# Local attention on one core: keys-first weights between the projection's halves, outputs turned in front of queries and keys, the halo scaled early

## The chip, the cores and the metric

The kernel runs on one core of a Trainium2 chip as one program. The metric is device time in microseconds (us). Before the change three runs took 5033.6, 5040.5 and 5043.14 us, median 5040.5.

## The reference, cut to what matters

Two stages, each with a first half (attention of its own kind) and a second half of local-attention layers. The change touches the second halves only: 6 layers of 16 heads with windows of 32 tokens (stage L0), then 2 layers of 8 heads with windows of 64 (stage L1). The data are 2 sequences of 2048 tokens by 128 features there, all in fp32. One layer computes:

```python
h = shift_token(x)                       # half of the features come from the token before
q, k, v = split(h @ Wqkv)                # heads of 64
q, k = l2norm(q) * qs, l2norm(k) * ks
q, k = rotary(q) * scale, rotary(k) / scale
sim = 8 * q_window @ [k_previous_window, k_window].T   # masked
o = softmax(sim) @ [v_previous_window, v_window]
x = x + o @ Wo
h = layernorm(shift_token(x))            # feed-forward
x = x + ((h @ Wa + ba) * gelu(h @ Wg + bg)) @ W2 + b2
```

L1's first half (a causal linear attention with its own feed-forward) is computed block by block among the tiles at the seam between the two stages.

## The kernel before, in words

After L0's first half, `local_models` walks through 256 tiles: 8 layers, 16 tiles of 128 tokens, 2 sequences (the sequence is the inner loop). Activations stay in SBUF with features on partitions (`hs`). Each tile goes through these steps, one function each; the names in brackets are the tiles that the profile shows.

- `project(j, u)` multiplies tokens by one kilocolumn of Wqkv (`ps_qk`, L871, four array passes of 512 columns). ScalarE squares the result (`sq`, L873), VectorE multiplies it by the rotary tables in two instructions (L881 into `r`, L886 into `t`), GpSimd adds the two (L892). L0 has two such halves (u = 0, 1: `nu` is 2), L1 one (`nu` is 1). After the last half VectorE reduces the squares (L897) and computes an inverse root in nine small instructions (L167 to L180, the result is `rq_y`, the scratch is the PSUM tile `ps_qk` itself); GpSimd scales `r` with it (L904).
- `values` projects V (`ps_v`, L951), ScalarE copies it out (`vn`, L952), and SyncE's DMA queue arranges windows in `v2` (L961 to L964, ten DMAs in an L0 tile).
- `turn` transposes queries and keys (`ps_turn`, L923); ScalarE copies them to `qT` and `kT` (L926, L928). Its end fills the keys' halo, the window before the tile, from the same sequence's last tile: one ScalarE activation that scales it (L934), or a memset by GpSimd at the start of a sequence (L932).
- `scores` puts the mask in PSUM with two bf16 matmuls (`ps_s`, L982), adds 64 small score products (L991; they use 64 by 32 parts of the array), and VectorE takes the maximum (L999) and subtracts it (L1001). `weights_exp` is ScalarE's exp (L1008), `weights_norm` a sum, a reciprocal (VectorE, L1015, L1016) and a scaling on GpSimd (L1017).
- `keys_first_` transposes the weights (`ps_pT`, L1026), and ScalarE copies them to `pT` in two instructions (L1027).
- `mix` multiplies weights with values (`ps_o`, L1043, again small array parts); ScalarE copies to `on` (L1049).
- `turn_out` transposes that (`ps_oT`, L1059), ScalarE copies to `oT` (L1060); `project_out` multiplies by Wo (`ps_y`, L1071), VectorE adds the residual (L1077).
- `feed_forward` queues six closures for each 512 tokens (`steps`): centre (`ps_c`, L1096, squared by ScalarE into `fsq`, L1098), variance (`ps_var`, L1107), scale (`ps_r`, L1120), gate and up (`ps_f`, L1141, with ScalarE's Gelu at L1151 and VectorE's product at L1158), down (`ps_fy`, L1166). Each round of the main loop takes two of them. `linear` and `output` queue closures of the seam and of the end in the same way (`lsteps`).

The tiles are software pipelined. Round i of the main loop computes the scores of tile i+1, the projection of tile i+3, weights, mix and output of tile i, and values and turning of tile i+2. Each round emits, in this order: scores(i+1) with exp and normalising; project(i+3, 0); one feed-forward step; project(i+3, 1) in L0 only; keys_first_(i) and values(i+2); mix(i) and turn(i+2); turn_out(i); one feed-forward step; project_out(i).

This is the order in which the source emits; a scheduler then gives each engine its own fixed order, which stays near the emitted one but lets a later instruction pass one that it expects to wait. Each engine runs its list strictly in order. PSUM is shared by two pools: `wide` (2 buffers of two banks: scores, projection halves, gate and up) and `bank` (4 buffers of one bank: everything else). A buffer comes free when its last reader is done. In SBUF, `pT` and `oT` share one buffer, `kT` has three, `vn` three, `v2` two.

Of the kernel before, what the change touches and what calls it, by code (L numbers as in the profile page):

```python
# [11 lines left out]
F32 = mybir.dt.float32  # L12
BF16 = mybir.dt.bfloat16
I32 = mybir.dt.int32
AF = mybir.ActivationFunctionType
# [57 lines left out]
def tile_kernel(ctx: ExitStack, tc: tile.TileContext, a: dict, out: bass.AP):  # L73
# [634 lines left out]
    def local_models(mA, mB, hs0):  # L708
# [141 lines left out]
        def tables(g, t):  # L850
            cs = wk.tile([128, 2, DH], F32, name="cs", bufs=2)
            nc.sync.dma_start(cs[:, 0], a["cos"][:, t, :])
            nc.sync.dma_start(cs[:, 1], a["sin"][:, t, :])
            tb = wk.tile([128, 2, 2, DH], F32, name="tb", bufs=3)
            for j in range(2):
                nc.gpsimd.tensor_tensor(
                    tb[:, j], fac[g][:, j], bc(cs[:, j].unsqueeze(1), (128, 2, DH)), ALU.mult
                )
            tabs[g, t] = tb


        def project(i, u):
            g, b, t = tiles[i]
            m, _ = layers[g]
            H, units = m.H, m.units
            tb = tabs[g, t]
            hw = hs[0][:, b, t * 128:(t + 1) * 128]
            pq = wide("qk")
            for j in range(2):
                js = slice(512 * j, 512 * j + 512)  # L870
                nc.tensor.matmul(pq[:, js], lhsT=hw, rhs=wts[g, u][:, js], start=True, stop=True)  # L871
            sq = wk.tile([128, 1024], F32, name="sq", bufs=2)
            nc.scalar.activation(sq, pq, AF.Square)  # L873
            r = wk.tile([128, 1024], F32, name=f"r{u}", bufs=2)
            t2 = wk.tile([128, 1024], F32, name="t2", bufs=1)
            same = units[u][0][0] == units[u][1][0]
            for e in range(1) if same else range(2):
                s = units[u][e][0]
                hn = 16 if same else 8
                es = slice(512 * e, 512 * e + 64 * hn)  # L880
                nc.vector.tensor_tensor(  # L881
                    r[:, es].rearrange("p (h d) -> p h d", d=DH),
                    pq[:, es].rearrange("p (h d) -> p h d", d=DH),
                    bc(tb[:, 0, s].unsqueeze(1), (128, hn, DH)), ALU.mult,
                )
                nc.vector.tensor_tensor(  # L886
                    t2[:, es].rearrange("p (h s d) -> p h s d", s=2, d=32),
                    pq[:, es].rearrange("p (h s d) -> p h s d", s=2, d=32)[:, :, ::-1, :],
                    bc(tb[:, 1, s].rearrange("p (s d) -> p s d", s=2).unsqueeze(1),
                       (128, hn, 2, 32)), ALU.mult,  # L890
                )
            nc.gpsimd.tensor_tensor(r, r, t2, ALU.add)  # L892
            st[i]["r", u], st[i]["sq", u] = r, sq
            if u == len(units) - 1:

                for v in range(len(units)):
                    nc.vector.tensor_reduce(  # L897
                        pq[:, 16 * v:16 * v + 16],
                        st[i].pop(("sq", v)).rearrange("p (h d) -> p h d", d=DH), AX.X, ALU.add,
                    )  # L900
                y = rsqrt_quick([pq[:, k * 32:k * 32 + 2 * H] for k in range(4)], 2 * H, wk)
                for v in range(len(units)):
                    rv = st[i]["r", v].rearrange("p (h d) -> p h d", d=DH)
                    nc.gpsimd.tensor_tensor(  # L904
                        rv, rv, bc(y[:, 16 * v:16 * v + 16].unsqueeze(2), (128, 16, DH)), ALU.mult
                    )

        def turn(i, u):

            g, b, t = tiles[i]  # L910
            m, _ = layers[g]
            W, NPR = m.W, m.NPR
            if u == 0:
                q = wk.tile([128, 1024], F32, name="qT")
                st[i]["q"] = q[:, 0:NPR * 128].rearrange("p (c i) -> p c i", c=NPR)
                k = wk.tile([128, 1280], F32, name="kT", bufs=3)
                st[i]["k"] = k[:, 0:NPR * (W + 128)].rearrange("p (c i) -> p c i", c=NPR)
            r = st[i].pop(("r", u))
            for e, (s, pb) in enumerate(m.units[u]):
                p = bank("turn")  # L920
                for c in range(4):
                    cs = slice(512 * e + 128 * c, 512 * e + 128 * c + 128)
                    nc.tensor.transpose(p[:, c * 128:(c + 1) * 128], r[:, cs], ident)  # L923
                pv = p.rearrange("p (c i) -> p c i", c=4)
                if s == 0:
                    nc.scalar.copy(st[i]["q"][:, 4 * pb:4 * pb + 4, :], pv)  # L926
                else:
                    nc.scalar.copy(st[i]["k"][:, 4 * pb:4 * pb + 4, W:W + 128], pv)  # L928
            if u == len(m.units) - 1:
                k = st[i]["k"]  # L930
                if t == 0:
                    nc.gpsimd.memset(k[:, :, 0:W], 0.0)  # L932
                else:
                    nc.scalar.activation(  # L934
                        k[:, :, 0:W], m.last_k[b][:, :, 128:128 + W], AF.Identity, scale=m.back
                    )
                m.last_k[b] = k

        def values(i):
            g, b, t = tiles[i]  # L940
# [78 lines left out]
        def keys_first_(i):  # L1019
            sm = st[i].pop("p")  # L1020
            pT = wk.tile([128, 2, 4, 128], F32, tag="pT", name="pT")
            for q in range(2):
                p = bank("pT")
                for c in range(4):
                    cs = slice(512 * q + 128 * c, 512 * q + 128 * c + 128)
                    nc.tensor.transpose(p[:, c * 128:(c + 1) * 128], sm[:, cs], ident)  # L1026
                nc.scalar.copy(pT[:, q].rearrange("p c i -> p (c i)"), p)  # L1027
            st[i]["pT"] = pT
# [60 lines left out]
        def lstep():  # L1089
            if lsteps:  # L1090
                lsteps.pop(0)()
# [362 lines left out]
        for i in range(-3, n):  # L1454
            j = i + 3
            lstep()
            if 0 <= i + 1 < n:
                scores(i + 1)
                weights_exp(i + 1)
                weights_norm(i + 1)  # L1460
            more = False
            if j < n:
                g, b, t = tiles[j]
                jj = j % per
                nu = len(layers[g][0].units)
                more = g < last
                if g == second and t % 4 == 0:
                    while (b, t // 4) not in ready:
                        lstep()
                project(j, 0)  # L1470
                if more and jj == 4:
                    load_proj(g + 1, 0)
                if more and jj == 6 and g + 1 == second:
                    models[1].consts()
                if jj == 6 and g == second - 1:
                    linear_consts()
                if more and jj == 8:
                    factors(g + 1)
                    if 2 == 2:
                        load_out(g + 1)  # L1480
                if more and jj == 18:
                    load_ff(g + 1)
                if more and jj == 22:
                    fold_ff(g + 1)
                if more and jj == per - 1:
                    load_proj(g + 1, 1)
                lstep()
            step()
            if j < n and nu == 2:
                project(j, 1)  # L1490
                if more and jj == per - 1 and g + 1 < second:
                    load_proj(g + 1, 2)
            if j < n and b == B - 1 and j + 1 < n:
                tables(*tiles[j + 1][::2])
            lstep()
            if i >= 0:
                keys_first_(i)
            if 0 <= i + 2 < n:
                values(i + 2)
            lstep()  # L1500
            if i >= 0:
                mix(i)
            if 0 <= i + 2 < n:
                for u in range(len(layers[tiles[i + 2][0]][0].units)):
                    turn(i + 2, u)
            lstep()
            if i >= 0:
                turn_out(i)
            step()
            lstep()  # L1510
            if i >= 0:
                g, b, t = tiles[i]
                project_out(i)
                if 2 == 1 and i % per == per - 1 and g < last:
                    load_out(g + 1)
                if t % 4 == 3:
                    feed_forward(g, b, t // 4)
# [74 lines left out]
```

## Time and profile before

| what | value |
| --- | --- |
| three runs | 5033.6, 5040.5, 5043.14 us |
| profiled execution, its own time | 5053.27 us |
| its span, first to last instruction | 5051.4 us |
| granted TensorE clock, mean | 0.959 |
| stretch 650 to 3590 us (L0's layers): granted clock | 1.00 |
| in that stretch of 2940 us, busy: TensorE / VectorE / ScalarE / GpSimd | 2878.59 / 2379.62 / 1794.23 / 1870.56 us |
| stretch 3590 to 4400 us (seam with the linear attention): clock, TensorE / VectorE busy of 810 us | 0.96, 752.90 / 554.02 us |
| stretch 4400 to 5052 us (L1's layers alone): clock, TensorE / VectorE busy of 652 us | 0.98, 602.36 / 516.60 us |

How to read the profile. PE is TensorE's matmuls, PEld its weight loads, DVE VectorE, ACT ScalarE, POOL GpSimd, SP the DMA-issuing SyncE. "ps_o<-v,pT" is the output and inputs of an instruction, "L1043" its line. A busy TensorE isn't TensorE at its peak: matmuls overlap, and the times used below are therefore the distances between the starts of consecutive groups. The profiled execution took 12.8 us more than the median of the three runs.

### The profile page before, as it was taken

How to read it: one execution, taken by the hardware profiler on the slowest of the kernel's cores; microseconds unless marked ns; L12 is line 12 of the kernel's file. 1: busy time of each engine (PE TensorE's matmuls, PEld its weight loads, DVE VectorE, ACT ScalarE, POOL GpSimd, SP SyncE). 2: the span in 40 equal slices, each digit the busy share in tenths (PEclk: the TensorE clock that was granted, in tenths of full speed). 3: DMA queues.
4: the chain of work that ended last, by engine and by line, in shares of the span. 5: the costliest groups of instructions: out<-in, count | busy, mean ns of one | idle time of the engine just before them, and what ended most of it. 6: DMA issues, size and time to landing. Idle time of an engine off the chain costs nothing.

```text
span 5051.4 us, 171478 instructions
## 1 busy us (share of the span) xinstructions
PE 4682.5 (93%) x75042; PEld 3190.3 (63%) x75042; DVE 3883.5 (77%) x6760; ACT 2796.3 (55%) x4645; POOL 2761.1 (55%) x1650
## 2 busy tenths in 40 slices
PE   5667799999999999999999999999999998999998
PEld 4445566666666666666666666666666665566565
DVE  6993488788887887788887788787767766688886
ACT  3323356666666665566665566566555654555554
POOL 3331366666665666566666666665544533355553
PEclk8777799999999999999999999999999999999999
DMA  2000222222222322232222322232222211111111
GB/s 76 1 1 24 83 69 66 63 71 74 70 63 63 82 70 63 62 81 72 63 64 65 81 67 64 64 82 64 52 53 54 54 44 36 41 46 48 53 54 40
DMA packets 222491, 295.63 MB, mean 59 GB/s; under 512 B 75657, under 2 KB 95409, under 8 KB 221745
## 3 DMA queue, kind: packets, MB, share of 16 engines
q1 hardware_dynamic: 221744, 284.67, 21.8%
q8 instruction: 592, 9.70, 0.8%
q14 instruction: 155, 1.26, 0.1%
HBM read 40.98 MB, written 10.75 MB: 10 GB/s over the span
## 4 chain that ended last, share of the span: by engine, by line
PE 75%; DVE 6%; ACT 4%; issue 2%; POOL 2%; DMA 0%; SPq 0%; ACTq 0%; POOLq 0%; DVEq 0%
PE ps_qk L871 15%; PE ps_y L1071 8%; PE ps_turn L923 8%; PE ps_o L1043 7%; PE ps_s L991 7%; PE ps_v L951 6%; PE ps_f L1141 6%; PE ps_oT L1059 4%; PE ps_pT L1026 4%; PE ps_fy L1166 3%; PE ps_var L1107 1%; PE ps_c L1096 1%; PE ps_s L982 1%; POOL r L892 1%; ACT sq L873 1%
## 5 line engine op out<-in xcount | busy, mean ns | idle before, releaser
L892 POOL TENSOR_TENSOR r<-r,t 128x1024 f32<-128x1024 f32 x448 | 1059.9, 2366 | 1162.4 <-DVE t L886 1075.2
L873 ACT ACTIVATE sq<-ps_qk 128x1024 f32<-128x1024 f32 x448 | 459.1, 1025 | 1369.4 <-PE ps_qk L871 1353.2
L904 POOL TENSOR_TENSOR r<-r,rq_y 128x1024 f32<-128x1024 f32 x448 | 845.5, 1905 | 268.0 <-DVE rq_y L180 267.1
L871 PE MATMUL ps_qk<-wp,hs 128*128 128x512 f32 x1792 | 883.6, 616 | 30.1 <-DVE rq_y L180 15.4
L886 DVE TENSOR_TENSOR t<-ps_qk,tb 128x1024 f32<-128x1024 f32 (+1 forms) x512 | 552.8, 1080 | 180.5 <-POOL r L892 180.4
L1017 POOL TENSOR_TENSOR sm<-sm,rs 128x1024 f32<-128x1024 f32 x256 | 488.0, 1906 | 293.6 <-DVE rs L1016 196.2
L881 DVE TENSOR_TENSOR r<-ps_qk,tb 128x1024 f32<-128x1024 f32 (+1 forms) x512 | 547.7, 1070 | 103.1 <-ACT sq L873 102.1
L897 DVE TENSOR_REDUCE ps_qk<-sq 128x16 f32<-128x1024 f32 x448 | 549.6, 1227 | 13.5
L871 PEld LDWEIGHTS ps_qk<-wp,hs 128*128 128x128 f32 x1792 | 311.6, 191 | 351.5 <-issue 260.2
L1071 PEld LDWEIGHTS ps_y<-oT,wo 128*128 128x128 f32 x3584 | 440.8, 193 | 122.4 <-issue 71.1
L1071 PE MATMUL ps_y<-oT,wo 128*128 128x128 f32 x3584 | 482.8, 282 | 18.7 <-ACT oT L1060 18.2
L923 PE MATMUL ps_turn<-ident,r 128*128 128x128 f32 x3584 | 470.6, 281 | 22.9 <-issue 12.0
L1043 PEld LDWEIGHTS ps_o<-v,pT 64*32 64x32 f32 (+1 forms) x26624 | 343.6, 108 | 226.9 <-ACT pT L1027 114.9
L951 PE MATMUL ps_v<-wp,hs 128*128 128x512 f32 x896 | 446.9, 598 | 5.9 <-ACT o L1436 3.7
L999 DVE TENSOR_REDUCE mx<-ps_s 128x16 f32<-128x1024 f32 (+1 forms) x256 | 312.9, 1222 | 166.4 <-PE ps_s L991 162.1
L1043 PE MATMUL ps_o<-v,pT 64*32 64x64 f32 (+1 forms) x26624 | 392.5, 222 | 41.0 <-ACT pT L1027 23.3
L923 PEld LDWEIGHTS ps_turn<-ident,r 128*128 128x128 f32 x3584 | 395.2, 143 | 54.4 <-issue 15.8
L991 PE MATMUL ps_s<-kT,qT 64*32 64x64 f32 (+1 forms) x26624 | 400.5, 230 | 3.9 <-ACT kT L928 3.2
L1049 ACT COPY on<-ps_o 128x512 f32<-128x512 f32 x448 | 244.4, 589 | 244.1 <-PE ps_o L1043 244.1
L991 PEld LDWEIGHTS ps_s<-kT,qT 64*32 64x32 f32 (+1 forms) x26624 | 330.1, 107 | 70.3 <-issue 37.3
L1141 PE MATMUL ps_f<-fx,w 128*128 128x512 f32 (+1 forms) x768 | 365.5, 600 | 2.6 <-DVE fx L1123 1.7
L1026 PEld LDWEIGHTS ps_pT<-ident,sm 128*128 128x128 f32 x2048 | 245.7, 142 | 149.6 <-issue 142.1
(266 smaller groups left out, 7693.6 us busy)
## 6 DMA issues: line engine op xcount, KB each, us to landing
v<-vn SPq DMA_DIRECT2D x1276, 128.0 KB
v<-vn SPq DMA_DIRECT2D x744, 64.0 KB
v<-vn SPq DMA_DIRECT2D x64, 256.0 KB
wp<-in_L_ffn_Wqkv SPq DMA_DIRECT2D x20, 512.0 KB
xD<-xb SPq DMA_DIRECT2D x24, 256.0 KB
xb<-xD SPq DMA_DIRECT2D x24, 256.0 KB
cs<-in_cos SPq DMA_DIRECT2D x128, 32.0 KB
cs<-in_sin SPq DMA_DIRECT2D x128, 32.0 KB
```

Of the source, the lines that this page charges most:

```text
L871: nc.tensor.matmul(pq[:, js], lhsT=hw, rhs=wts[g, u][:, js], start=True, stop=True)
L881: nc.vector.tensor_tensor(r[:, es].rearrange("p (h d) -> p h d", d=DH), pq[:, es].rearrange("p (h d) -> p h d", d=DH), bc(tb[:, 0, s].unsq ...
L886: nc.vector.tensor_tensor(t2[:, es].rearrange("p (h s d) -> p h s d", s=2, d=32), pq[:, es].rearrange("p (h s d) -> p h s d", s=2, d=32)[: ...
L892: nc.gpsimd.tensor_tensor(r, r, t2, ALU.add)
L897: nc.vector.tensor_reduce(pq[:, 16 * v:16 * v + 16], st[i].pop(("sq", v)).rearrange("p (h d) -> p h d", d=DH), AX.X, ALU.add,)
L904: nc.gpsimd.tensor_tensor(rv, rv, bc(y[:, 16 * v:16 * v + 16].unsqueeze(2), (128, 16, DH)), ALU.mult)
L923: nc.tensor.transpose(p[:, c * 128:(c + 1) * 128], r[:, cs], ident)
L951: nc.tensor.matmul(p, lhsT=hw, rhs=wv, start=True, stop=True)
L991: nc.tensor.matmul(sp[W * w:W * w + W, c0:c0 + 2 * W], lhsT=qT[64 * q:64 * q + 64, cc, W * w:W * w + W], rhs=kT[64 * q:64 * q + 64, cc, W ...
L1043: nc.tensor.matmul(po[s][W * w:W * w + W, co:co + 64], lhsT=pT[kp, q, c, W * w:W * w + W], rhs=v2[kp, w, co:co + 64], start=True, stop=True,)
L1071: nc.tensor.matmul(py[:, 0:128], lhsT=wts[g, "o"][:, c * NO + s, :], rhs=oT[:, s, c, :], start=(c + s == 0), stop=(c == 3 and s == NO - 1),)
L1141: nc.tensor.matmul(ps_[c][0:sz], lhsT=wts[g, "w1"][:, o:o + sz], rhs=S["x"], start=True, stop=True,)
```

## The change

The emitted order of a round is changed, and the halo becomes a function of its own:

- `keys_first_(i)` moves from behind the second projection half to between the two halves (in L1: in front of the only one, which itself moves from the round's start to this place).
- `values(i+2)` moves from in front of `mix(i)` to behind it.
- `turn_out(i)` moves from behind `turn(i+2)` to in front of it.
- The halo of tile i+2's keys is scaled (or set to zero) in front of the second projection half, no longer at the end of `turn`; `kT` is claimed there too.

No instruction is added or removed. The order of the loads of Wqkv is kept (the one of L1 moves with its projection).

```diff
+        def halo(i):
+
+            g, b, t = tiles[i]
+            m, _ = layers[g]
+            W, NPR = m.W, m.NPR
+            k = wk.tile([128, 1280], F32, name="kT", bufs=3)
+            k = st[i]["k"] = k[:, 0:NPR * (W + 128)].rearrange("p (c i) -> p c i", c=NPR)
+            if t == 0:
+                nc.gpsimd.memset(k[:, :, 0:W], 0.0)
+            else:
+                nc.scalar.activation(
+                    k[:, :, 0:W], m.last_k[b][:, :, 128:128 + W], AF.Identity, scale=m.back
+                )
+            m.last_k[b] = k
+
...
-                project(j, 0)
+                if nu == 2:
+                    project(j, 0)
...
             step()
-            if j < n and nu == 2:
-                project(j, 1)
+            if i >= 0:
+                keys_first_(i)
+            if 0 <= i + 2 < n:
+                halo(i + 2)
+            if j < n:
+                project(j, nu - 1)
...
             lstep()
             if i >= 0:
-                keys_first_(i)
+                mix(i)
+            lstep()
             if 0 <= i + 2 < n:
                 values(i + 2)
             lstep()
             if i >= 0:
-                mix(i)
+                turn_out(i)
             if 0 <= i + 2 < n:
                 for u in range(len(layers[tiles[i + 2][0]][0].units)):
                     turn(i + 2, u)
-            lstep()
-            if i >= 0:
-                turn_out(i)
             step()
```

More of the change, by code (lines that the diff above doesn't have):

```diff
@@ L915, in turn @@
                 st[i]["q"] = q[:, 0:NPR * 128].rearrange("p (c i) -> p c i", c=NPR)
-                k = wk.tile([128, 1280], F32, name="kT", bufs=3)
-                st[i]["k"] = k[:, 0:NPR * (W + 128)].rearrange("p (c i) -> p c i", c=NPR)
             r = st[i].pop(("r", u))
@@ L928, in turn @@
                     nc.scalar.copy(st[i]["k"][:, 4 * pb:4 * pb + 4, W:W + 128], pv)
[L929 to L937, printed above, removed]
         def values(i):
@@ L1484, in local_models @@
                     fold_ff(g + 1)
-                if more and jj == per - 1:
+                if nu == 2 and more and jj == per - 1:
                     load_proj(g + 1, 1)
@@ L1488, in local_models @@
             step()
-            if j < n and nu == 2:
-                project(j, 1)
-                if more and jj == per - 1 and g + 1 < second:
+            if i >= 0:
[4 more added lines that the diff above has]
+                project(j, nu - 1)
+                if nu == 2 and more and jj == per - 1 and g + 1 < second:
                     load_proj(g + 1, 2)
-            if j < n and b == B - 1 and j + 1 < n:
-                tables(*tiles[j + 1][::2])
+                if nu == 1 and more and jj == per - 1:
+                    load_proj(g + 1, 1)
+                if b == B - 1 and j + 1 < n:
+                    tables(*tiles[j + 1][::2])
             lstep()
             if i >= 0:
-                keys_first_(i)
+                mix(i)
+            lstep()
             if 0 <= i + 2 < n:
```

## Prediction

> **What bounds the kernel now.** First the page's head and its chain of the work that ended last.
>
> ```profile
> span 5051.4 us, 171478 instructions
> ...
> PE 4682.5 (93%) x75042; PEld 3190.3 (63%) x75042; DVE 3883.5 (77%) x6760; ACT 2796.3 (55%) x4645; POOL 2761.1 (55%) x1650
> ...
> PE 75%; DVE 6%; ACT 4%; issue 2%; POOL 2%; DMA 0%; SPq 0%; ACTq 0%; POOLq 0%; DVEq 0%
> ```
>
> TensorE carries the chain and no single line does. The change adds no work, so it can only save pauses of TensorE or make new ones. I therefore read TensorE's timeline in L0, where 192 of the 256 tiles lie (650 to 3590 us), and measure each group from its start to the next group's start. Time zero of a tile is the start of its first projection half. Two feed-forwards of three rounds each fall on 8 tiles, so there are four kinds of tiles, two of each in 8: **c** (centre, later variance), **r** (scale, later gate), **f** (up, later down), **plain**. Their lengths, medians over L0's timeline: plain 15.19, c 16.47, r 17.04, f 19.24 us. The end of a c tile:
>
> ```profile
> 2198.99 1.57 PE L1043 MATMUL ps_o<-v,pT 64*32 64x64 f32 x128
> 2200.49 1.96 PE L923 MATMUL ps_turn<-ident,r 128*128 128x128 f32 x16
> 2202.29 1.04 PE L1059 MATMUL ps_oT<-ident,on 128*128 128x128 f32 x8
> 2203.17 0.95 PE L1107 MATMUL ps_var<-onesm,fsq 128*128 128x1 f32 x8
> 2204.05 0.39 PE L982 MATMUL ps_s<-L_maskb,pick 64*128 64x512 bf16 x2
> 2204.37 0.49 PE L1071 MATMUL ps_y<-oT,wo 128*128 128x128 f32 x2
> 2204.79 0.30 PE L991 MATMUL ps_s<-kT,qT 64*32 64x64 f32 x2
> 2205.01 1.83 PE L1071 MATMUL ps_y<-oT,wo 128*128 128x128 f32 x14
> 2206.77 1.57 PE L991 MATMUL ps_s<-kT,qT 64*32 64x64 f32 x126
> 2208.27 1.98 PE L871 MATMUL ps_qk<-wp,hs 128*128 128x512 f32 x4
> ```
>
> Scores and ps_y are cut into each other: ps_y takes 0.42 + 1.76 = 2.18 us and the scores 0.22 + 1.50 = 1.72. In an r or f tile, where they stand in one piece (2171.23 for the scores, 2188.26 for ps_y), they take 1.88 and 1.41. The cuts cost 0.6 us: each change from small array parts to the whole array and back. ps_y is late because ScalarE's copies of oT come last behind six others; in plain tiles it also pauses outright, as the waits of 650 to 3590 us say, next to other pauses behind ps_o:
>
> ```profile
> PE ps_y L1071 <- ACT oT L1060: 15.7, 42, 0.4
> PE ps_turn L923 <- issue: 12.0, 12, 2.4
> ```
>
> **The change, part by part.** The order of the built instructions is known. In L0 it is, for every kind: ps_qk, (c, r or f), ps_pT, ps_qk, ps_o, ps_v, ps_oT, ps_turn, (var, f or fy), ps_y, mask, scores. ps_y and scores are no longer cut. In f tiles alone five of ps_o's products stand in front of the second ps_qk. ScalarE's list is sq, exp, (fsq), both pT copies, sq, on, vn, oT, turn's copies, halo; VectorE's list in L0 is unchanged.
>
> *What is exposed.* ps_o needs pT. Before, ps_v, ps_qk and ps_v (3.5 us) lay between ps_pT and ps_o; now only ps_qk does (1.72 and 0.09 for the change to small parts). The pT copies stand behind exp. In an f tile that is late, since ScalarE reloads exp's table after Gelu:
>
> ```profile
> 2174.66 1.02 ACT L873 ACTIVATE sq<-ps_qk 128x1024 f32<-128x1024 f32 x1 [3.39 <-PE ps_qk L871]
> 2175.71 1.28 ACT L1008 ACT_TABLE_LOAD   x1
> 2177.00 1.06 ACT L1008 ACTIVATE sm<-sm 128x1024 f32<-128x1024 f32 x1
> 2177.97 1.05 ACT L1027 COPY pT<-ps_pT 128x512 f32<-128x512 f32 x2
> ```
>
> With zero at 2172.64, exp runs from 4.36 to 5.42 and the first copy ends near 5.89. ps_pT ends at 5.29 on TensorE. Before, ps_v filled the gap. Now ps_o waits, and all of TensorE's list behind it: five products at 5.99 (0.1 for the semaphore, as ps_o trails pT elsewhere), 0.20 with the return to the whole array, ps_qk 1.81, rest of ps_o 1.45, ps_v 1.72, oT 0.87, turn 1.75: done at 13.79 instead of 13.03. **f: +0.75** (bounds +0.5, if ps_o needs neither latency nor change of parts, and +1.3, if the five wait for the second copy too).
>
> A rule of the Trainium skill speaks harder against the change here: "ScalarE: Activation LUTs", section "What ACT_TABLE_LOAD costs", puts a switch at 1.28 us for the load and 1.38 for a drain. The trace has exp 0.01 us behind the load's end. By the page an f tile would lose 1.38 more, 66 us over 48 tiles; I keep to the trace.
>
> *c.* TensorE alone: 1.82 + 0.86 + 0.87 + 1.81 + 1.50 + 1.72 + 0.87 + 1.75 + 0.88 + 1.88 + 0.32 + 1.42 = 15.70. exp ends at 3.99 (median), fsq and the copies follow, the second ends near 5.47; ps_o would start at 5.36, so 0.2 is lost: 15.9. **c: -0.55** (bounds -0.75 and -0.1).
>
> *r.* The copies end at 4.95 (the median in plain tiles, where ScalarE has this order already); ps_o starts at 4.94. 16.97: **r: -0.07** (bounds -0.1 and +0.5).
>
> *plain.* TensorE alone needs 14.45. But the next first half reuses the second half's PSUM buffer, which rq_y frees. rq_y ends at 14.82, behind a chain that starts with the maximum at 0.11 and isn't shortened: 14.9. **plain: -0.27** (0 and -0.35). So VectorE's chain is late next, and takes two thirds of what TensorE saves.
>
> Sum over 48 tiles of each kind: 36 - 26 - 3 - 13 = **-6 us**.
>
> *Turning later.* ps_turn starts 2.6 us (ps_v and ps_oT) later after ps_o than before. Its pauses (12.0 "issue", 2.9 for qT, 0.7 for r) may be covered in part by ps_v: -4; bounds -16, and +20 if pauses of that sort move in front of the scores.
>
> *At nothing.* The halo (0.56 us of ScalarE, 240 times) and the memset (0.32 us of GpSimd, 16 times): the built list has the halo behind turn's copies and in front of sq, which idles for ps_qk there (3.4 to 6.9 us); without that cover it is 0.56 on 180 tiles, 101 us in L0. kT's third buffer is free by then, since the scores of the tile that held it are done. vn and its ten DMAs leave about 1.8 us later; they issue for 6.5 us and are read two tiles (30 us) later. Behind them on SP wait the table loads (cs) for the next tile and weights, both a tile or more ahead. If a landing did bind, the nearest row is ps_o's own "issue" waits, up to 2.6 us, which would come per tile. turn's copies to qT follow the scores that read it. PSUM: turn's first two buffers wait for vn's copies (2.4 us after ps_o, needed at 2.6), the next for oT's (2.95, needed at 3.5): close, but covered.
>
> *L1.* At the seam, 32 tiles, TensorE is interleaved with much else: 0 (bounds -10 and +15). In the last 32 tiles the 8-tile cycle takes 97.7 us (4553.39 to 4651.09), and VectorE is busy for 82.45 of it. Moving the projection behind ps_pT delays sq and L881. By hand, plain and c tiles stay equal within 0.4. In r tiles, ps_r now stands directly behind the scores and waits for the inverse root on GpSimd (1.01 us, listed behind L892's 2.35); pT, exp and the gate's buffer follow late, 13.8 instead of 12.3. 8 r tiles by 1.5: **+12 us** (bounds -10 and +35).
>
> Total -6 - 4 + 12 = +2. Against the profiled execution that is 5053.3 + 2 = 5055; it took 12.8 us more than the median, which I take to hold for the kernel after as well: **5042 us**.
>
> **Rivals.**
> *Slower, by the pT copies.* If the subtraction (L1001) ends later than 2.59, exp and with it the copies slip, and c, r and f tiles pay in full; it decides from the point where VectorE starts the maximum more than 0.3 us after the scores end, which the freed TensorE can cause after plain tiles. For: plain tiles leave VectorE 0.5 behind; only one list position holds pT behind exp. Against: L881 waits 0.4 to 0.5 for sq anyway, which absorbs a lag. 0.25 us on 144 tiles is 36: 5078.
> *Faster.* The gains of c and plain hold, L1 costs nothing, and ps_turn's pauses vanish: -6 - 16 = -22: 5018.
> *The scheduler cuts ps_y again.* The built list rules that out for L0: a mask is followed by a whole-array group 96 times before, 5 times after.
>
> **How the numbers follow.** About 0.2% (10 us) is what a measurement can tell here. Forecast (terms cancel, 5027 to 5057): 0.40; slower rival (5057 to 5100): 0.35; faster rival (4995 to 5027): 0.25. From these: faster 0.30, same 0.30, slower 0.40. The unknown ends together reach further; I leave out a tenth on either side: 5003 to 5088.
>
> **What would show it.** Right: ps_y as one group of 16 at 1.88 us; PE ps_y no longer waits for oT; a new TensorE wait of ps_o for pT, near 0.7 us in f tiles; lengths 14.9, 15.9, 17.0, 20.0. Wrong: ps_o waiting 0.3 us or more in r tiles, plain tiles still 15.19, L1's cycle away from 101, or new "issue" waits before the scores.

## The result, and the profile after

The changed kernel takes 5078.13 us (median of 6 runs, 5071.09 to 5089.75), the kernel before 5041.82 us (6 runs): 36 us more, a ratio of 1.0073 with a 95% interval of 1.0057 to 1.0089. The profiled execution took 5076.48 us, close to its median, while that of before had been 12.8 us over its own.

Head and chain of the page of the changed kernel:

```profile
span 5074.7 us, 171165 instructions
...
PE 4652.6 (92%) x75042; PEld 3172.6 (63%) x75042; DVE 3885.1 (77%) x6760; ACT 2853.6 (56%) x4645; POOL 2763.3 (54%) x1650
...
PE 64%; DVE 11%; ACT 6%; POOL 4%; issue 3%; DMA 1%; SPq 0%; POOLq 0%; DVEq 0%; ACTq 0%
```

TensorE is busy for 30 us less than before, yet the span is longer. Its share of the chain fell from 75% to 64%; VectorE's went from 6% to 11% and GpSimd's from 2% to 4%. Cutting TensorE's own work short exposed other engines. The end of a c tile, from the timeline of TensorE:

```profile
2061.11 1.04 PE L1063 MATMUL ps_oT<-ident,on 128*128 128x128 f32 x8
2061.99 1.91 PE L936 MATMUL ps_turn<-ident,r 128*128 128x128 f32 x16
2063.74 0.95 PE L1111 MATMUL ps_var<-onesm,fsq 128*128 128x1 f32 x8
2064.55 2.03 PE L1075 MATMUL ps_y<-oT,wo 128*128 128x128 f32 x16
2066.51 0.39 PE L986 MATMUL ps_s<-L_maskb,pick 64*128 64x512 bf16 x2
2066.83 1.48 PE L995 MATMUL ps_s<-kT,qT 64*32 64x64 f32 x128
2068.24 1.13 PE L871 MATMUL ps_qk<-wp,hs 128*128 128x512 f32 x2
```

ps_y is one group of 16 and the 128 score products are one group too: neither is cut any more. ps_y takes 1.96 us to the mask's start and the scores 1.41, where before they took 2.18 and 1.72. The waits of TensorE from 650 to 3590 us:

```profile
PE ps_o L1047 <- issue: 21.2, 17, 2.0
PE ps_o L1047 <- ACT pT L1031: 19.8, 41, 0.5
PE ps_qk L871 <- DVE rq_y L180: 19.3, 22, 2.9
PE ps_qk L871 <- DVE sm L1005: 5.2, 19, 0.6
```

ps_y's waits for oT and ps_turn's pauses are gone from the list. In their place ps_o waits for pT, once in each of 41 f tiles, and the projection waits for VectorE.

**Where the 36 us are.** I cut the trace at the mask's first matmul of tiles 0, 176, 190 and 208: L0's regular tiles, L0's last 14 (the linear attention's closures are queued there), the handover and L1's first 16 tiles, and the rest of L1. Lengths in us, one profiled execution each; the experiments explained below are included.

| kernel | to tile 0 | 0 to 176 | 176 to 190 | 190 to 208 | 208 to end | median of runs |
| --- | --- | --- | --- | --- | --- | --- |
| before | 610.8 | 3086.9 | 354.7 | 355.3 | 643.8 | 5041.8 |
| after | 604.6 | 3086.4 | 373.1 | 349.0 | 661.6 | 5078.1 |
| l0_new | 600.3 | 3084.4 | 373.2 | 351.8 | 643.9 | 5055.9 |
| l1_new | 599.9 | 3084.3 | 354.5 | 350.5 | 658.0 | 5048.6 |
| l0_split | 605.1 | 3044.5 | 368.7 | 361.9 | 646.4 | 5023.3 |
| l1_proj | 601.2 | 3083.5 | 351.9 | 340.4 | 658.7 | 5030.3 |
| l0_pure | 602.0 | 3089.5 | 356.0 | 351.9 | 648.3 | 5048.8 |
| l0_keys | 599.5 | 3076.6 | 353.4 | 353.5 | 646.2 | 5029.5 |
| l0_out | 598.5 | 3087.3 | 355.5 | 348.9 | 646.2 | 5041.3 |
| l0_lstep | 597.8 | 3084.3 | 350.1 | 356.2 | 648.5 | 5034.8 |
| l1_step | 605.5 | 3089.5 | 352.6 | 331.3 | 653.5 | 5024.6 |
| best | 598.1 | 3044.7 | 352.7 | 338.0 | 648.0 | 4986.5 |
| best_halo | 596.7 | 3041.6 | 352.7 | 334.6 | 647.7 | 4979.7 |
| best_lstep | 599.5 | 3043.8 | 342.3 | 334.5 | 647.9 | 4986.0 |

Nothing is won or lost in L0's regular tiles (l1_proj and l1_step have the same order there and differ by 6 us, so a smaller difference says nothing). The price is paid in two places with few tiles: 18 us in the last 14 tiles of L0 and 18 us in L1 from tile 208 on; the handover gives 6 back. That is some 29 of the 36 us; the rest is in no stretch of these two profiles. The column to tile 0 holds no changed code. Its 610.8 in the profile of before is 5 to 14 us above all others, at a granted clock of 0.76 against 0.78 to 0.81. So most of that execution's surplus of 12.8 us was in front of the layers, and comparing the two profiled executions (+23 us) understates the change.

The stretches also differ in the granted TensorE clock, which the lengths don't show. From 0 to 176 it is 0.99 in every profile. The others:

| granted clock | 176 to 190 | 190 to 208 | 208 to end |
| --- | --- | --- | --- |
| before | 0.97 | 0.93 | 0.99 |
| after | 0.96 | 0.95 | 0.98 |
| l0_new | 0.96 | 0.94 | 0.99 |
| l1_new | 0.98 | 0.94 | 0.99 |
| l0_lstep | 1.00 | 0.93 | 0.98 |
| l1_proj | 0.98 | 0.96 | 0.97 |
| l1_step | 0.98 | 0.97 | 0.97 |

Length times clock is an estimate of a stretch at the full clock, and too low where TensorE waits anyway. By it the handover takes 330 us before and 332 after: the 6 us that it gives back are clock. The 18 us of each of the other two places stay for the most part.

### The profile page after: what moved, and what is told of

Read it like the earlier page. It is cut to its first block, busy times and chain, and to the rows that moved or that the text cites. A ratio compares the mean times of both kernels' runs of the same rounds, so it can differ in the third digit from the quotient of the medians.

```text
span 5074.7 us, 171165 instructions
## 1 busy us (share of the span) xinstructions
PE 4652.6 (92%) x75042; PEld 3172.6 (63%) x75042; DVE 3885.1 (77%) x6760; ACT 2853.6 (56%) x4645; POOL 2763.3 (54%) x1650
## 4 chain that ended last, share of the span: by engine, by line
PE 64%; DVE 11%; ACT 6%; POOL 4%; issue 3%; DMA 1%; SPq 0%; POOLq 0%; DVEq 0%; ACTq 0%
PE ps_qk L871 13%; PE ps_v L955 7%; PE ps_y L1075 6%; PE ps_turn L936 6%; PE ps_o L1047 6%; PE ps_s L995 5%; PE ps_f L1145 4%; PE ps_oT L1063 3%; PE ps_fy L1170 3%; POOL r L892 3%; PE ps_pT L1030 2%; DVE t L886 2%; DVE ps_qk L897 2%; ACT sq L873 2%; DVE r L881 2%
## 5 line engine op out<-in xcount | busy, mean ns | idle before, releaser
L1047 PEld LDWEIGHTS ps_o<-v,pT 64*32 64x32 f32 (+1 forms) x26624 | 356.5, 108 | 287.4 <-ACT pT L1031 162.9
L1047 PE MATMUL ps_o<-v,pT 64*32 64x64 f32 (+1 forms) x26624 | 421.8, 223 | 57.3 <-ACT pT L1031 32.3
L955 PE MATMUL ps_v<-wp,hs 128*128 128x512 f32 x896 | 462.7, 633 | 2.0 <-issue 1.6
L1075 PE MATMUL ps_y<-oT,wo 128*128 128x128 f32 x3584 | 452.2, 278 | 1.3 <-ACT oT L1064 1.2
L936 PE MATMUL ps_turn<-ident,r 128*128 128x128 f32 x3584 | 442.2, 275 | 5.8 <-POOL r L904 4.4
L936 PEld LDWEIGHTS ps_turn<-ident,r 128*128 128x128 f32 x3584 | 405.8, 143 | 10.5 <-POOL r L904 7.1
L1031 ACT COPY pT<-ps_pT 128x512 f32<-128x512 f32 x512 | 274.4, 586 | 168.4 <-PE ps_pT L1030 168.4
L1019 DVE TENSOR_REDUCE rs<-sm 128x16 f32<-128x1024 f32 (+1 forms) x256 | 309.9, 1211 | 76.2 <-ACT sm L1012 75.9
L995 PE MATMUL ps_s<-kT,qT 64*32 64x64 f32 (+1 forms) x26624 | 363.6, 229 | 0.6 <-issue 0.6
L995 PEld LDWEIGHTS ps_s<-kT,qT 64*32 64x32 f32 (+1 forms) x26624 | 315.2, 107 | 63.3 <-issue 49.2
```

Of the source, the lines that this page charges most:

```text
L955: nc.tensor.matmul(p, lhsT=hw, rhs=wv, start=True, stop=True)
L995: nc.tensor.matmul(sp[W * w:W * w + W, c0:c0 + 2 * W], lhsT=qT[64 * q:64 * q + 64, cc, W * w:W * w + W], rhs=kT[64 * q:64 * q + 64, cc, W ...
L1047: nc.tensor.matmul(po[s][W * w:W * w + W, co:co + 64], lhsT=pT[kp, q, c, W * w:W * w + W], rhs=v2[kp, w, co:co + 64], start=True, stop=True,)
L1075: nc.tensor.matmul(py[:, 0:128], lhsT=wts[g, "o"][:, c * NO + s, :], rhs=oT[:, s, c, :], start=(c + s == 0), stop=(c == 3 and s == NO - 1),)
```

## The experiments

The median of before on the chips that ran them was 5039 to 5044 us; each ratio is against before on the same chip.

### The new order in one stage only: l0_new and l1_new

```diff
 # l0_new; in l1_new the branches are exchanged
+if j < n and nu == 2:
+    new_order()   # keys_first_, halo, project, mix, values, turn_out, turn
+else:
+    old_order()   # project, keys_first_, values, mix, turn, turn_out
```

> The new order in L0's rounds (projection of L0 tiles), the old one in all rounds of L1 (seam and last tiles). Theory A, the price is paid in L1: in the two profiled executions L0's layers end at the same distance from their start, the seam is some 12 us longer and L1's last tiles some 18 us; so this kernel stands at the kernel before or a little below: 5035 us (5025 to 5045). Theory B, the price is paid in L0, by ps_o waiting for pT behind exp and by pauses marked issue: 5065 to 5080.

Measured: 5055.86 us, ratio 1.0032 (1.0020 to 1.0044).

> The old order in L0, the new one in L1's rounds alone. Theory A (price in L1): 5070 to 5080, that is 30 us or more over the kernel before. Theory B (price in L0): within 10 us of the kernel before, 5035 to 5052.

Measured: 5048.60 us, ratio 1.0016 (1.0007 to 1.0025).

Neither theory holds alone: the halves cost 17 and 9 us, together 26 of the 36, and the table says where. l0_new loses nothing between tiles 0 and 176 but 18 us between 176 and 190. l1_new loses 14 us from 208 to the end and wins 5 at the handover. So "in L0" and "in L1" was the wrong cut: the question was regular tiles or tiles among other work.

### More cover in front of ps_o in L0: l0_split

```diff
 # to l0_new
+values(i + 2, [0])     # first of the two ps_v products, with its copy
 mix(i)
-values(i + 2)
+values(i + 2, [1])     # the second, and the DMAs to v2
```

> As l0_new, but values is split in L0: one of its two products stands in front of ps_o, one behind it, so that ps_o has 0.86 us more of cover for pT's copies, and on's copies keep 0.86 us in front of ps_oT. L1 has the old order. If the exposed pT copies are the only thing that eats the gain of the uncut ps_y in L0, f tiles go from 20.2 back to about 19.3 us, c tiles to 15.7, r and plain tiles stay at 17.0 and 14.9: 48 times (0.1 - 0.75 - 0.1 - 0.3) = -50 us against the kernel before, 4990 us (4980 to 5005). If pauses marked issue take the gain, whatever stands in front of ps_o, 5025 to 5045.

Measured: 5023.26 us, ratio 0.9966 (0.9954 to 0.9979). The regular tiles take 3044.5 us, 32 to 45 us less than in the kernels with values in one piece. The total misses both forecasts, the second by 2 us: the regular tiles gain 42 us against before where 50 were expected, and the last 14 tiles and the handover lose 21 of it. An f tile of the changed kernel, first TensorE, then ScalarE:

```profile
2179.34 0.27 PE L1030 MATMUL ps_pT<-ident,sm 128*128 128x128 f32 x1
2179.45 1.90 PE L1145 MATMUL ps_f<-fx,w 128*128 128x512 f32 x4
2181.18 0.93 PE L1030 MATMUL ps_pT<-ident,sm 128*128 128x128 f32 x7
2182.60 0.39 PE L1047 MATMUL ps_o<-v,pT 64*32 64x64 f32 x10 [0.49 <-ACT pT L1031]
2182.93 1.98 PE L871 MATMUL ps_qk<-wp,hs 128*128 128x512 f32 x4
2184.84 1.45 PE L1047 MATMUL ps_o<-v,pT 64*32 64x64 f32 x118
```

```profile
2178.68 1.03 ACT L873 ACTIVATE sq<-ps_qk 128x1024 f32<-128x1024 f32 x1 [3.43 <-PE ps_qk L871]
2179.72 1.28 ACT L1012 ACT_TABLE_LOAD   x1
2181.02 1.06 ACT L1012 ACTIVATE sm<-sm 128x1024 f32<-128x1024 f32 x1
2181.98 1.06 ACT L1031 COPY pT<-ps_pT 128x512 f32<-128x512 f32 x2
```

ps_pT ends at 2182.11. The first pT copy stands behind the table load and exp and ends near 2182.5; the ten matmuls of five products begin at 2182.60, the second projection half only at 2182.93. The same place in l0_split:

```profile
2150.06 0.93 PE L1046 MATMUL ps_pT<-ident,sm 128*128 128x128 f32 x7
2150.82 1.02 PE L969 MATMUL ps_v<-wp,hs 128*128 128x512 f32 x2
2151.69 1.92 PE L871 MATMUL ps_qk<-wp,hs 128*128 128x512 f32 x4
2153.53 1.57 PE L1063 MATMUL ps_o<-v,pT 64*32 64x64 f32 x128
```

Here half of ps_v and the projection half fill the gap, and ps_o stands in one piece behind the copies. Medians of the four kinds:

| kernel | plain | c | r | f |
| --- | --- | --- | --- | --- |
| before | 15.19 | 16.45 | 17.04 | 19.24 |
| after | 14.87 | 16.00 | 17.12 | 20.19 |
| l0_split | 14.87 | 15.93 | 17.08 | 19.28 |

The f tiles get their 0.9 us back and plain and c keep their gains. In L0's regular tiles the exposed pT copies, with the cut through ps_o that goes with them, were what ate the gain.

### The projection behind ps_pT in L1: l1_proj

```diff
 # to before, rounds with nu == 1 only
-project(j, 0)
...
 step()
 keys_first_(i)
+project(j, 0)
 values(i + 2)
```

> The old order everywhere, but in L1's rounds the only projection stands behind ps_pT (in front of values) instead of at the round's start. Theory A1, the price of L1 comes from this move (ps_r then directly behind the scores, waiting for frt on GpSimd): 5060 to 5078. Theory A2, it comes from values and turn_out changing places (ps_oT then waits for on's copies, 17 us in the profile of after): within 10 us of the kernel before, 5035 to 5052.

Measured: 5030.27 us, ratio 0.9984 (0.9975 to 0.9993). The median says neither theory; the stages explain it. From 208 to the end this one move costs as much as the whole new order (658.7 us against 658.0 in l1_new, old 643.8). That doesn't make the two prices the same: the clock there is 0.97 against 0.99, which by an estimate (0.02 of 658.7) can make up to 13 of the 15 us, and to tile 236 the move costs 10 us and the whole order 6, from there to tile 255 it costs 8 and the whole order 16. From 190 to 208 it wins 10 to 15 us. By length times clock 3 of the 15 are left (327 against 330), and why the clock is higher isn't shown. The source lets the projection of an L1 tile wait there for the linear attention's result; that other steps now go ahead of it is an argument, not a finding. The waits of TensorE from 4410 to 4980 us, before:

```profile
PE ps_o L1043 <- ACT pT L1027: 16.4, 26, 1.7
PE ps_v L951 <- ACT o L1436: 3.7, 3, 1.2
```

and in l1_proj:

```profile
PE ps_turn L945 <- POOL r L904: 10.7, 10, 1.9
PE ps_r L1135 <- POOL frt L1129: 9.2, 10, 1.2
PE ps_out L1447 <- issue: 8.0, 4, 2.3
PE ps_out L1447 <- DVE xb L1202: 4.6, 2, 2.3
```

The move takes away ps_o's waits for pT and ps_v's for o, 20.1 us, and puts three others in their place: ps_turn for an r that is scaled late because its projection was late (10.7), ps_r for frt (9.2), and ps_out (12.6 together; to the end of the kernel 17.2, where before it was 5.9). The changed kernel has another list in the same window:

```profile
PE ps_oT L1063 <- ACT on L1053: 15.3, 24, 0.9
PE ps_r L1124 <- POOL frt L1118: 10.1, 10, 1.3
PE ps_o L1047 <- ACT pT L1031: 9.0, 24, 1.2
```

Its longest wait, of ps_oT for on's copies, comes with the exchange of values and turn_out, and l1_proj doesn't have it. So how much of L1's price the late projection makes by itself stays open. Ps_out belongs to the closures fetch, residual and leave, which put the results out: without the projection between them two lstep calls stand only the scores apart. One r tile of l1_proj shows the wait for frt:

```profile
4592.86 0.89 PE L1006 MATMUL ps_s<-kT,qT 64*64 64x128 f32 x24
4594.76 0.65 PE L1135 MATMUL ps_r<-ident,frt 128*128 128x128 f32 x4 [1.01 <-POOL frt L1129]
4595.24 0.93 PE L1041 MATMUL ps_pT<-ident,sm 128*128 128x128 f32 x7
```

ps_r is next behind the scores and stands idle for 1.01 us; the ps_pT behind it could have run in that time.

### A feed-forward step behind ps_pT: l1_step

```diff
 # to l1_proj, rounds with nu == 1
-step()
 keys_first_(i)
+step()
 project(j, 0)
```

> As l1_proj, but in L1's rounds the feed-forward's step stands behind the turning of the weights and in front of the projection, so that 0.87 us of ps_pT lie between the scores and ps_r. Theory: ps_r standing directly behind the scores (9.2 us of waits for frt between 4410 and 4980 us in l1_proj) is a good part of L1's price: from tile 208 to the end 659 falls to 646 to 652 us, the kernel to 5020 us (5014 to 5025). Rival, the late projection itself is the price (r is ready late for ps_turn, 10.7 us there): 5028 us or more.

Measured: 5024.55 us, ratio 0.9963 (0.9952 to 0.9974); 208 to the end 653.5 us. About a third of l1_proj's price (5 of 15 us) goes, less than I expected for this stretch; the total falls into the theory's range with a handover of 331.3 us, the shortest in the table, at a clock of 0.97. The waits in the same stretch:

```profile
PE ps_turn L945 <- POOL r L904: 17.1, 18, 1.9
PE ps_out L1447 <- issue: 7.6, 4, 2.2
PE ps_out L1447 <- DVE xb L1202: 3.9, 2, 1.9
```

ps_r's wait is gone, and ps_turn's wait for r has grown from 10.7 to 17.1 us: the projection is now later still. ps_out's waits are as they were. Both theories hold a part, and ps_r's is the smaller one. Whether the closures' places alone explain ps_out, as they do at the seam, was not tried.

### The old order among the closures: l0_pure

```diff
 # to l0_new
-if j < n and nu == 2:
+if j < n and nu == 2 and not lsteps:
```

> As l0_new, but a round keeps the old order as long as closures of the linear attention are queued, so the last 14 or so tiles of L0 run as before. Between the scores of tile 176 and those of tile 190 the profiles of the old order in L0 show 352 to 355 us, those of the new order 373. Theory S, the price of l0_new (17 us) sits there: 5038 us (5030 to 5046), equal to the kernel before. Rival, the price sits in the regular tiles of L0: 5050 to 5060.

Measured: 5048.80 us, ratio 1.0012 (1.0002 to 1.0021), between the two forecasts. The stretch itself did what theory S said (356.0 us instead of 373.2). The rest of this profile is longer than l0_new's by 2 us in front of the layers and by 4 to 5 in two other stages, and no single place accounts for the remaining 10 us.

### The closures' places: l0_lstep

```diff
 # to l0_new
 mix(i)
-lstep()
 values(i + 2)
 lstep()
 turn_out(i)
 turn(i + 2)
+lstep()
 step()
```

> As l0_new, but the closure of the linear attention that the change put between mix and values is taken behind turn (mix, values, closure, turn_out, turn, closure), so that at least 2.6 us of a round's own work lie between two closures again. Theory: the 19 us between tiles 176 and 190 come from this place (variance and its reader only ps_v apart, so ps_r waits for frt: 13.2 us there in l0_new, 7.0 with the old order): that stretch falls from 373 to some 360 us, the kernel to 5041 us (5035 to 5047). Rival, it is the order of the tiles' own steps among the closures: 5050 to 5060.

Measured: 5034.81 us, ratio 0.9988 (0.9979 to 0.9997): 21 us less than l0_new for the place of one call. Tiles 176 to 190 take 350.1 us. The waits of TensorE from 3685 to 4058 us, in l0_new:

```profile
PE ps_r L1135 <- POOL frt L1129: 13.2, 5, 4.5
PE ps_oT L1074 <- DVE h L1406: 2.3, 1, 2.3
PE ps_o L1058 <- issue: 2.1, 1, 2.1
```

and in l0_lstep:

```profile
PE ps_r L1135 <- POOL frt L1129: 4.4, 5, 1.5
PE ps_qk L871 <- DVE sm L1016: 2.5, 2, 1.4
```

With the old order (l1_new) the first line says 7.0 us. The diff had left the number of lstep calls as it was but put one between mix and values, so that variance and the ps_r that reads it came to lie one ps_v apart. Frt is made on GpSimd, behind whatever is queued there. One such place in l0_new:

```profile
3785.98 1.05 PE L1122 MATMUL ps_var<-onesm,fsq 128*128 128x1 f32 x8
3786.89 1.96 PE L966 MATMUL ps_v<-wp,hs 128*128 128x512 f32 x4
3791.68 0.96 PE L1135 MATMUL ps_r<-ident,frt 128*128 128x128 f32 x4 [2.83 <-POOL frt L1129]
3792.44 1.91 PE L1074 MATMUL ps_oT<-ident,on 128*128 128x128 f32 x8
```

The place of that one call was the seam's price, but not by the waits alone: they fall by 8.8 us and the stretch by 23. The rest can be clock. In the rows above ps_oT takes 1.91 us instead of 1.04, and from 3792 to 3795 us the granted clock is 0.50. Over the stretch it is 0.96 in l0_new and 1.00 in l0_lstep, by an estimate (0.04 of 373.2) up to 15 us. Whether the waits cause the lower clock is suggested by such rows and not shown. By length times clock l0_lstep takes 350 us and the kernels with the old order 344 to 348, so it isn't better than they are.

### Two parts alone: l0_keys and l0_out

```diff
 # l0_keys, to before; in L0 while no closure is queued
+keys_first_(i)
 project(j, 1)
-keys_first_(i)
 values(i + 2)
 # l0_out, to before; the same rounds
 mix(i)
+turn_out(i)
 turn(i + 2)
-turn_out(i)
```

> Of the change only its first part, in L0's rounds without closures: the weights are turned between the projection's halves, and all else stays in the old order. The built list of TensorE had ps_pT there in most tiles already, and ps_v still stands in front of ps_o: within 5 us of the kernel before, 5034 to 5044. Rival, pT's copies in front of the second sq delay VectorE's L881: 5048 or more.

Measured: 5029.47 us, ratio 0.9982 (0.9971 to 0.9992), 5 us better than the range I gave. In c tiles ps_pT is no longer split around the projection (16.37 against 16.45), and the six r tiles that also fold weights or constants take 19.4 instead of 20.2. That is 8 us together, of some 10.

> Of the change only this part, in L0's rounds without closures: turn_out stands in front of turn, values stays in front of mix. ps_y is then uncut (a gain near 0.6 us in 96 plain and c tiles, 58 us), but ps_oT follows ps_o with nothing or the mask between, and waits for on's copies: some 0.5 to 0.7 us in 190 tiles, 95 to 130 us. Theory: 5075 to 5115. Rival, on's wait is covered (the mask, the other steps): 4985 to 5010.

Measured: 5041.27 us, ratio 0.9999 (0.9990 to 1.0008). Both theories miss. The built list puts the mask between ps_o and ps_oT, and on's wait is only 26.1 us in 113 tiles, 0.23 each. Against before, plain tiles win 0.32 us, f tiles lose 0.33, c and r change by 0.05. The gains of this part and its price cancel; in l0_split, with half of values behind mix as well, plain tiles keep the gain and f tiles pay nothing.

### The parts that pay, together: best, best_halo, best_lstep

```diff
 # best
+if j < n and nu == 2 and not lsteps:   # order of l0_split
...
+elif j < n and g == second:            # order of l1_proj, L1's first layer
...
+else:                                  # old order
...
 # best_halo, to best: the halo stays at the end of turn
-halo(i + 2)
 # best_lstep, to best_halo: closures as in l0_lstep, to the end of L0
-if j < n and nu == 2 and not lsteps:
+if j < n and nu == 2:
...
 mix(i)
-lstep()
 values(i + 2, [1])
...
 turn(i + 2)
+lstep()
```

> Values split around mix in L0 (as l0_split) while no closure of the linear attention is queued, the old order otherwise; in L1's first layer the projection behind ps_pT (as l1_proj), in its second layer the old order. Sum of the stages, each from the profile that shows it: 605 to the first scores, 3044.5 to tile 176 (l0_split), 352 to tile 190 and 29 to tile 192 (l1_proj), 311 to tile 208 (l1_proj), 645 to the end (kernel before), with 2 around the span: 4989 us (4978 to 5000). Rival, the stages are not free of each other and pauses come back elsewhere: 5005 to 5025.

Measured: 4986.51 us, ratio 0.9893 (0.9877 to 0.9909), 52.7 us under before and 2.5 from the sum of the stages. The stages add up. Of the gain 17 us lie in the handover, where the granted clock is 0.96 against 0.93.

> As best, but the halo stays at the end of turn. The halo was costed at nothing: within 6 us of best, 4980 to 4993 us. Rival, the early halo takes 0.56 us of ScalarE in front of something late (or frees it): 10 us or more away from best.

Measured: 4979.74 us, ratio 0.9878 (0.9864 to 0.9893). 6.8 us under best, just outside what I gave, with intervals that overlap: the early halo gains nothing, and if it does anything, it costs.

> As best_halo, but the split order holds to the end of L0, with the linear attention's closures placed as in l0_lstep, instead of the old order while closures are queued. In l0_lstep tiles 176 to 190 took 350 us, in best_halo, with the old order there, 353; the split might save 2 or 3 more. Theory: 4976 us (4970 to 4982). Rival, the old order is the better one among the closures: 4985 or more.

Measured: 4985.96 us, ratio 0.9889 (0.9873 to 0.9906). Its profiled execution has 342.3 us from tile 176 to 190, the shortest of all, but that execution is the fastest of four and the median is not lower. Inconclusive; best_halo stays the best.

What binds next in best_halo, from 640 to 3580 us:

```profile
PE ps_qk L871 <- DVE rq_y L180: 38.0, 43, 3.7
PE ps_o L1048 <- issue: 16.0, 11, 2.5
```

The projection waits for VectorE's chain in nearly every plain tile, as the prediction said would be late next.

## Why the prediction was right or wrong

The forecast was +2 us, measured were +36. The time lies inside the range and at the price of the slower rival, and both are luck: neither the forecast's sum nor the rival's mechanism made it. By the stretches of the two profiles L0's regular tiles gave nothing instead of -10, the seam +12 instead of 0 and L1 +18 instead of +12.

- **ps_y uncut.** Right: one group of 16, no wait for oT; c -0.45 (-0.55 forecast) and plain -0.32 (-0.27) in medians.
- **What is exposed, f.** Right in mechanism, 0.2 small: +0.95, not +0.75. ps_o starts 5.94 us after the tile's start (forecast 5.99), and its wait is 0.5, not near 0.7. The miss is behind it: five products with the return to the whole array take 0.33, not 0.20; ps_qk 1.91, not 1.81; ps_v 1.82, not 1.72. Each of these three is 0.10 to 0.13 over, as if a change of parts stood in each place, where I had counted it once.
- **r.** +0.08 instead of -0.07: ps_o takes 1.55 instead of 1.50, no wait of 0.3 as the rival wanted. With c and f this is 0.1 to 0.2 a tile, in the rival's direction and under its 0.25. But exp and the copies did not slip, as the rival needs: ps_o starts at 5.37 (c), 4.94 (r) and 5.94 (f), where I had 5.56, 4.94 and 5.99.
- **The table load.** The Trainium skill, "ScalarE: Activation LUTs", section "What ACT_TABLE_LOAD costs", would add 1.38 us of drain to each switch. In the f tile above the load takes 1.28 us, starts 0.01 behind the instruction in front of it, and exp starts 0.02 behind its end: no drain shows. The trace decides, as the prediction took it.
- **Turning later, -4.** ps_turn's 12.0 us of pauses went. But ps_o's moved from f tiles (seven, 2.4 us each over the median) to plain tiles (ten, 2.0 each), and ps_v pauses five times by 1.2 behind them. The mean of plain tiles rose from 15.50 to 15.79 us while the median fell. In sum such pauses fell from 38 to 28 us, more than the -4 I gave.
- **L0 in sum.** -10 was forecast. The profiles of the new order (after, l0_new, l0_pure, l0_lstep) have 3084 to 3090 us from tile 0 to 176; those of the old one (before, l1_new, l1_proj, l1_step) 3084 to 3090 too. Zero. By medians 44 f tiles pay 42 us and the other kinds together win 30; the pauses are 10 us less. So the f tiles, forecast at +0.75 each, took what c, plain and the pauses gave.
- **The seam, 0 (bounds -10 and +15).** This is the step that failed by omission. I treated lstep as not moved because the count of calls is the same. L0's last 14 tiles pay 18 us, and moving one call takes all of it away again (l0_lstep), in part through the granted clock; the handover gives 6 back, by clock. The sum of +12 is inside the bounds, for a reason that the prediction didn't have.
- **L1, +12.** The mechanism named is there: ps_r waits for frt behind the scores. It is one of several, since ps_oT's wait for on's copies, 15.3 us, stood nowhere in the sum. The last 32 tiles, for which the term was, grew by 16 us, and from tile 208 on it is 18. The term covered r tiles of the regular cycle only. There it was near enough: 8 tiles take 100.1 us (220 to 228) where I gave 101. Tiles 236 to 255, with output's closures among them, grew from 237.3 to 253.7 us, and I had not looked at those. Ps_out's pauses marked issue, 1.3 us behind 4800 us before, are 8.1 there now.
- **12.8 us over the median.** I took that to hold for the kernel after as well. It did not: most of it lay in front of the layers, in that one execution and at its lower clock, and the next profile sat at its own median.
- **The halo at nothing.** Within what could be measured (best against best_halo), at most some us of cost.

## What to carry to other kernels

When steps are reordered to end a wait, write down for each engine what stood between a result and its reader and still stands there afterwards: here one of two products put back in front of ps_o turned nothing into a gain of 40 us in L0's regular tiles. Calls that drain a queue of closures are steps too: moving one past a step changes the distance between a producer and its reader even if nothing else changes. And price the stages with few tiles as carefully as the regular ones: some 60 tiles out of 256 paid the whole price that the profiles show. Before a difference of a few us between two stretches is explained, compare the clock that was granted in them.

## What the runs showed of the hardware

The pauses that the profile marks as issue follow the order of the code, not the amount of work. Counted as what ps_o, ps_v, ps_oT and ps_turn take over their kind's median, by more than 0.8 us a tile, they are 38 us in L0's regular tiles before (15 of 23 in f tiles, behind ps_o and ps_turn; 36 to 45 in the three other profiles with that order), 28 with the new order (15 of 17 in plain tiles; 27 to 30 in the three others) and some 30 in l0_split, back in f tiles.

The traces say more of the longer ones. One DMA queue, q8, moves instructions: 592 packets of 16 KB, against 150,084 matmuls and weight loads, some 253 to a packet. From 650 to 3590 us TensorE has 15 issue pauses of over 0.8 us before, 11 after and 8 in l0_split, and each of them ends 1.1 to 1.6 us after such a packet has ended. Moments chosen at random lie that far behind a packet in 3 to 8% of cases. So the pauses look like TensorE waiting for its own instructions; no run varied that alone, and a proof is missing.

Where the granted clock is 0.5, TensorE's groups take nearly twice as long: from 3758 to 3761 us of l0_new (0.51) the four matmuls of ps_v take 3.56 us, at 3786.89 1.96.
